# Wider table rows, idle TensorE products ahead of the first batch, and a new order of all steps in a graph-attention kernel

## The chip, the cores and the metric

The kernel runs on one core of one Trainium2 chip. The metric is the device time of one execution in microseconds (us); lower is better. Engines are named as in the profile: PE is TensorE (PEld its weight loads), DVE is VectorE, ACT is ScalarE, POOL is GpSimd and SP is SyncE, which here only issues DMAs.

## The reference

The input x is (32, 512, 1024): 32 batches of 512 channels by 1024 nodes, in float32. adj is a 512 x 512 matrix. Cut to what matters:

```python
# layer 0: attention over the nodes
h = relu(layernorm(x))                            # over the 1024 nodes
q = einsum('c,bcn->bn', wq, h); k = einsum('c,bcn->bn', wk, h)
scores = q[:, None, :] + k[:, :, None]            # (b, m, n)
scores = where(scores > 0, scores, 0.01 * scores)
att = softmax(scores, axis=-1)
agg = einsum('bcn,bmn->bcm', h, att)
x = x + relu(einsum('oc,bcm->bom', adj, agg) + bm[None, :, None])
# layer 1: graph convolution over the channels
h = relu(layernorm(x))
x = x + einsum('bnf,nm->bmf', h, adj * adj) + bias
```

## The kernel before

A score is one number of the row plus one of the column, with a kink at zero. So the kernel never forms the 1024 x 1024 scores. It sorts the nodes by q and keeps running sums of weighted values over the sorted nodes. For each column it then looks up where the kink falls, and joins two running sums. The work of one batch goes through these steps, each a small function:

- load (L578) brings the four x tiles of 128 x 1024. stats, norm, slopes and relu make h of layer 0.
- scores (L625) makes q and k (tile pq). It writes q to DRAM (qd), and row reads it back onto all partitions (qrow). columns (L641, L646) turns q and k into columns (pr, qk).
- rank (L667 to L676, on DVE) counts for every node how many q lie below it. lower (L683, on ACT) finds for every column where its kink falls. to_rows and from_rows make table rows of these numbers, and factors makes the exponents.
- value (L724) multiplies h by the turned adjacency (wmT) into tile pv, spread copies pv to SBUF (v, L731). scatter, on POOL, adds one column with q (L736) and writes the 128 rows of v to their sorted places in a table in DRAM (td, L737, indirect DMA).
- fetch (L753) reads the sorted rows back (vs). weights, later, totals and stationary make the weights (w, wc, e, den, sm; the products pd at L785 and L786).
- scan (L812, L809) makes running sums of the sorted rows in nine pieces (sc). sums carries the last row of a piece into the next ones (vs, L821, L822) and copies the piece with its column of den to t (L824, L825), which SP writes into the table (L827, L828).
- gather (L833, POOL, indirect DMA) fetches for every column three neighbouring table rows (g). excess, divide, weigh and combine (L842 to L862) join them. turn (L869, L871) transposes the result (tr) and adds it to a fresh copy of x that reload (L583) brought (y).
- stats, norm, slopes, relu and lift handle layer 1. propagate (L876) multiplies by the squared adjacency (wsq, tile pg), and finish (L884, L888) adds and writes out.

Steps of up to six batches are in flight at once, and the order in which they are issued is written out. PLAN gives every step of a batch a time, FIRST and LAST shift and stretch these times for the first and the last six batches. Batch s.b adds s.b x T, with T = 80.647:

```python
shift, stretch = FIRST[name][s.b]
t = s.b * T + t + shift + stretch * (t - mean)
...
steps.sort(key=lambda e: e[:2])
with tc.manual_schedule():
    for _, _, f, args in steps:
        f(*args)
```

These times only sort; no engine waits for them. Every engine and every DMA queue takes its instructions in the resulting order. The setup steps run once: adjacency loads adj, turn_adjacency (L533, tile pt) transposes it and ACT copies it to wmT (L534), square makes wsq on POOL, and pads fills the table places that no node takes. ident, the identity for transposes, is made by POOL at the very start. TABLES = 5 tables are used in turn, and each table row has W = C + 1 = 513 floats, 512 values and one more for q or den. PSUM has 8 banks of 128 x 512 floats, handed out in turn by bank().

Of the kernel before, what the change touches and what calls it, by code (L numbers as in the profile page):

```python
# [16 lines left out]
P = 128  # L17
# [6 lines left out]
FAR = -1.0e30  # L24
# [4 lines left out]
    "adjacency": (-988.26,),  # L29
    "biases": (-98.417,),  # L30
    "columns": (-36.55,),
    "combine": (
        258.562, 258.888, 261.232, 259.873, 259.273, 258.008, 255.401, 254.706, 263.584, 262.603,
        263.336, 256.739, 262.598, 262.619, 257.172, 258.38,
    ),
    "compare_mask": (-790.92,),
    "divide": (245.486,),
    "excess": (235.359,),
    "factors": (7.808,),
    "fetch": (33.445,),  # L40
    "finish": (320.504, 328.605, 338.372, 339.335, 347.583, 375.553, 352.541, 377.322),
    "from_rows": (59.35,),
    "gather": (219.377, 220.155, 219.449, 220.224, 220.347, 220.229, 219.664, 221.598),
    "later": (44.625,),
    "lift": (323.119, 320.65, 321.319, 325.518),
    "load0": (-153.915,),
    "load1": (-113.779,),
    "load2": (-165.384,),
    "load3": (-89.604,),
    "lower": (-8.757, 10.345, -12.887, -23.448, -21.118, -20.974, -1.148, 2.379),  # L50
    "masks": (-130.916,),
    "norm0": (-78.759,),
    "norm1": (284.555,),
    "pads": (-161.502, -74.73, -204.361, 23.867, -54.392),
    "propagate": (312.313, 317.412, 326.151, 316.354, 335.303, 344.312, 335.972, 347.511),
    "rank": (-14.187, -14.293, -17.198, -17.342, -15.511, -15.036, -11.325, -13.895),
    "reload0": (192.65,),
    "reload1": (238.382,),
    "reload2": (232.99,),
    "reload3": (257.454,),  # L60
    "relu0": (-61.287, -58.703, -61.202, -57.828),
    "relu1": (301.878, 303.027, 301.741, 302.05),
    "row": (-36.021,),
    "scan": (51.176, 57.633, 64.219, 81.673, 97.074, 108.292, 133.694, 146.062, 161.601),
    "scatter": (20.023, 15.884, 17.044, 17.539, 21.356, 19.535, 20.598, 20.763),
    "scores": (-41.613,),
    "slopes0": (-64.705,),
    "slopes1": (285.486,),
    "spread": (-28.707, -25.435, -27.151, -16.385, -9.829, -20.617, -16.323, -10.067),
    "square": (-559.865,),  # L70
    "stationary": (45.131, 68.681, 108.55),
    "stats0": (-97.083, -80.936, -91.631, -79.428),
    "stats1": (279.045, 280.054, 279.907, 280.042),
    "sums": (51.891, 59.593, 72.069, 86.019, 99.75, 116.792, 139.403, 150.307, 173.296),
    "to_rows": (-11.86, -7.955),
    "totals": (50.392,),
    "turn0": (264.575, 264.492, 264.401, 264.843),
    "turn1": (269.122, 269.027, 269.324, 268.845),
    "turn_adjacency": (-328.788,),
    "value": (-34.236, -39.683, -34.816, -23.667, -14.904, -27.47, -22.782, -17.741),  # L80
    "weigh": (250.503, 251.121, 249.656, 248.481, 251.121, 249.301, 250.914, 250.078),
    "weights": (41.352,),
# [3 lines left out]
        (-34.664, 0.5139), (-50.924, 3.8424), (-25.352, -0.3814), (5.756, -0.7592),  # L86
        (-3.834, -3.5685), (-13.836, 0.3613),
    ),
    "combine": (
        (-10.962, -0.1119), (-1.308, -0.1439), (3.109, -1.7623), (9.89, 2.7475), (4.44, -0.7933),  # L90
        (2.961, -1.451),
    ),
    "divide": (
        (-6.347, -0.8568), (2.891, -3.3805), (-4.843, -2.2912), (-14.719, 0.1095), (0.139, -0.7459),
        (-4.639, -1.4913),
    ),
    "excess": (
        (3.406, 3.0798), (0.53, -2.1584), (-5.407, -3.6123), (-5.253, 0.2855), (1.538, 1.0506),
        (-3.02, -0.7059),
    ),  # L100
    "factors": (
        (-39.948, -1.434), (8.997, -3.1502), (-4.905, 1.5535), (21.711, -1.2202), (-25.661, 2.8879),
        (13.506, 1.2709),
    ),
    "fetch": (
        (-7.266, -0.8474), (-8.348, -0.3577), (-7.803, -0.4204), (-12.929, 0.9352),
        (-3.76, -1.7209), (-5.744, 2.9838),
    ),
    "finish": (
        (-8.493, -0.4813), (6.16, 0.0186), (3.358, -0.186), (-1.573, -0.1421), (1.288, 0.2274),  # L110
        (-7.871, -0.1255),
    ),
    "from_rows": (
        (-0.341, 2.1537), (116.48, -0.09), (-35.198, 1.4406), (-25.171, -1.3726), (0.332, 0.6924),
        (-16.655, 0.2663),
    ),
    "gather": (
        (-5.507, 0.5725), (-4.646, -0.3848), (-17.558, -0.6343), (-8.351, -0.483), (5.293, 1.8179),
        (-2.911, -0.6571),
    ),  # L120
    "later": (
        (-10.16, 1.3573), (-2.311, -1.2079), (-2.744, 1.4084), (-11.928, 2.0169), (-8.624, -2.2893),
        (0.485, -2.4426),
    ),
    "lift": (
        (-13.784, -1.0616), (3.658, -0.7922), (-29.558, 1.5668), (-5.824, -1.5872), (1.316, 0.2108),
        (-13.838, -1.4015),
    ),
    "load0": (
        (-175.071, -1.0804), (-56.257, 0.2897), (-197.902, -2.8166), (2.16, -0.6659),  # L130
        (-45.079, 1.0239), (23.433, -0.0172),
    ),
    "load1": (
        (-99.914, 2.1645), (-71.298, -3.9416), (-78.407, 2.8558), (-85.073, 0.4063),
        (-18.406, -0.1573), (-28.218, 0.3374),
    ),
    "load2": (
        (-70.747, -1.2538), (-111.83, -0.5989), (-26.701, -0.4923), (-111.109, -0.0099),
        (-20.511, 0.9791), (15.469, 0.2457),
    ),  # L140
    "load3": (
        (-206.722, 1.2803), (-128.427, -0.9745), (-37.172, 1.9538), (-74.142, 0.1775),
        (-13.958, 1.1538), (-37.508, 0.7277),
    ),
    "lower": (
        (-27.213, -0.696), (-36.917, 0.5414), (-27.222, -0.2022), (-13.712, -0.526),
        (-10.212, -0.0938), (46.957, -1.0187),
    ),
    "norm0": (
        (-82.445, 1.5089), (-65.85, -1.4094), (-21.204, -0.8537), (-14.029, -0.5842), (1.32, 1.776),  # L150
        (1.134, -0.2082),
    ),
    "norm1": (
        (-3.753, -0.8553), (7.036, 1.1487), (-3.41, 0.1137), (10.96, 0.1134), (5.687, 1.1579),
        (-1.719, -1.6549),
    ),
    "propagate": (
        (-0.512, -0.1834), (1.688, 0.0269), (-2.93, -0.0228), (-0.493, -0.1178), (0.476, -0.1272),
        (0.797, -0.0815),
    ),  # L160
    "rank": (
        (-18.998, 0.7993), (-32.202, -0.2074), (-19.965, 1.145), (-3.668, -1.203),
        (-5.408, -1.0875), (2.158, -0.1924),
    ),
    "reload0": (
        (-78.853, -1.3542), (-2.901, -0.2085), (48.545, 0.1436), (11.898, 1.3227),
        (28.811, -1.2219), (-1.29, -0.8095),
    ),
    "reload1": (
        (-41.749, 0.1112), (-10.749, -0.6043), (11.812, -1.0105), (7.019, -0.2259),  # L170
        (-60.814, -0.4054), (-89.384, 1.1482),
    ),
    "reload2": (
        (5.935, 0.7012), (9.237, 1.9026), (-112.445, -1.6665), (29.821, 0.2364), (-22.535, -0.3722),
        (10.909, 1.7943),
    ),
    "reload3": (
        (-10.61, -1.1804), (-7.721, -1.5967), (-28.859, -3.3307), (-19.113, 0.0501),
        (-9.413, 0.4983), (-16.835, 0.7363),
    ),  # L180
    "relu0": (
        (-60.02, 1.4731), (-66.989, -0.4028), (-18.196, 0.1369), (-19.764, 0.0603), (3.168, 0.0151),
        (-1.522, 0.1367),
    ),
    "relu1": (
        (-11.851, 2.5102), (-0.995, 1.8084), (-17.155, -2.1914), (1.666, 2.1743), (4.982, -0.4455),
        (3.476, 0.1775),
    ),
    "row": (
        (-58.902, 0.8165), (-32.755, -3.2129), (-16.685, -0.2803), (-0.884, 2.3638),  # L190
        (-10.929, 0.751), (-15.002, 1.1386),
    ),
    "scan": (
        (-5.392, -0.0092), (-4.281, 0.0691), (-9.753, -0.1007), (-4.67, 0.0238), (-1.515, -0.0228),
        (-2.326, 0.0007),
    ),
    "scatter": (
        (-9.248, -0.2038), (-2.595, 1.766), (5.273, -0.6066), (-14.049, -0.0507), (0.917, 1.0603),
        (-5.17, -0.1987),
    ),  # L200
    "scores": (
        (-62.678, -1.1751), (-58.023, -2.2273), (-24.037, 0.8897), (-9.373, 1.8513),
        (-9.692, 0.3259), (-10.3, 1.643),
    ),
    "slopes0": (
        (-59.101, 0.4464), (-71.353, -1.9588), (-30.833, -0.0625), (-22.09, 0.6177),
        (-7.677, 1.4505), (-7.382, -0.8102),
    ),
    "slopes1": (
        (-1.669, -0.6445), (12.184, -1.231), (-2.177, 0.2468), (12.041, 0.2135), (12.134, -1.0604),  # L210
        (1.475, -1.9438),
    ),
    "spread": (
        (1.755, 1.4749), (-14.586, -0.2764), (13.174, 0.6637), (10.836, 0.3786), (3.075, 0.789),
        (3.759, 0.7174),
    ),
    "stationary": (
        (-7.431, 0.0753), (2.851, 0.1776), (-11.126, -0.3907), (-4.759, 0.0962), (-1.682, 0.227),
        (-1.878, -0.1006),
# [224 lines left out]
def kernel(  # L444
# [32 lines left out]
    nc = tc.nc  # L477
    B, C, N = x.shape
# [89 lines left out]
    def bank(name):  # L568
        return ps.tile([P, HALF], F32, tag="bank", name=name)
# [401 lines left out]
```

## Time and profile before

| | |
|---|---|
| median of 3 runs | 2365.21 us (2362.98 to 2367.83) |
| the profiled execution | 2365.35 us, of which 2363.6 us are the span of its instructions |
| mean granted TensorE clock | 0.987 |
| busy, share of the span | PE 97%, DVE 83%, ACT 61%, POOL 31% |
| DMA | 643.59 MB, 272 GB/s on average; queue q1 (SP) 355.90 MB, q0 (POOL, indirect) 268.99 MB |
| chain that ended last | PE 78%, DVE 8%, DMA 7%, ACT 3% |

Lines of a timeline give the start and the length in us, the engine, the line of the kernel, the operation, the tile written and those read, and how many records. In brackets stands how long the engine sat idle before and what ended that. A product of float32 shows as two records, a transpose as one. Matmuls overlap, so the busy time of PE is not PE at its peak. The granted clock is the share of TensorE's full clock that the throttle let through.

### The profile page before, as it was taken

The page shows a single profiled execution, that of the slowest core. Times are in us where ns is not written, and L with a number is a line of the kernel's source. Part 1 is how long each engine was busy: PE and PEld are TensorE (multiplying, and loading weights), DVE is VectorE, ACT ScalarE, POOL GpSimd, SP SyncE. Part 2 cuts the span into 40 slices and gives each one's busy share as a digit, 9 for nine tenths or more (in the row PEclk, how much of TensorE's full clock was granted, in tenths as well). Part 3 has the DMA queues.
Part 4 walks back from the last instruction along what each step waited for, and adds up shares of the span by engine and source line. Part 5 has one row for each costly group of instructions (what it writes and reads, how often), then busy time and mean ns, then how long its engine had stood idle before and what let it go on. Part 6 is the DMA issues. An engine that isn't in the chain of part 4 may idle for free.

```text
span 2363.6 us, 27844 instructions
## 1 busy us (share of the span) xinstructions
PE 2290.4 (97%) x7568; PEld 1006.6 (43%) x7568; DVE 1954.1 (83%) x4981; ACT 1441.9 (61%) x2821; POOL 734.0 (31%) x971
## 2 busy tenths in 40 slices
PE   7898999999999999999999999999999999999997
PEld 3333444444444444444444444444444444444443
DVE  6557887898988888988888888888988896899875
ACT  4666666655766655666665666665676556676530
POOL 2233333233233223233323233323233333334310
PEclk8998999999999999999999999999999999999998
DMA  5779987988988898998898998889897898788971
GB/s 186 234 214 286 270 267 251 324 275 246 303 289 274 298 295 262 289 289 284 296 295 263 276 299 279 292 298 264 272 304 257 294 305 271 252 270 285 323 291 71
DMA packets 205356, 643.59 MB, mean 272 GB/s; under 512 B 27504, under 2 KB 27632, under 8 KB 205200
## 3 DMA queue, kind: packets, MB, share of 16 engines
q1 hardware_dynamic: 141408, 355.90, 50.6%
q0 software_dynamic: 57344, 268.99, 31.8%
q10 hardware_dynamic: 6448, 16.92, 2.2%
q8 instruction: 61, 1.00, 0.2%
q14 instruction: 95, 0.78, 0.1%
HBM read 429.94 MB, written 211.77 MB: 271 GB/s over the span
## 4 chain that ended last, share of the span: by engine, by line
PE 78%; DVE 8%; DMA 7%; ACT 3%; POOL 1%; issue 1%; SPq 0%; ACTq 0%; DVEq 0%; POOLq 0%
PE pg L876 31%; PE pv L724 31%; PE sc L812 8%; PE tr L869 4%; PE pq L625 2%; DMA vs<-td 2%; DVE st L591 2%; DMA g<-td,idg 1%; DVE g L862 1%; ACT junk L683 1%; DMA td<-t 1%; PE sc L809 1%; DMA td<-v,idx 1%; DVE junk L672 1%; ACT h L613 1%
## 5 line engine op out<-in xcount | busy, mean ns | idle before, releaser
L724 PE MATMUL pv<-wmT,x 128*128 128x512 f32 x2048 | 920.8, 601 | 0.7 <-DVE step L602 0.7
L876 PE MATMUL pg<-h,wsq 128*128 128x512 f32 x2048 | 907.0, 596 | 14.0 <-ACT h L613 12.8
L876 PEld LDWEIGHTS pg<-h,wsq 128*128 128x128 f32 x2048 | 385.0, 191 | 508.3 <-issue 466.7
L724 PEld LDWEIGHTS pv<-wmT,x 128*128 128x128 f32 x2048 | 378.9, 191 | 509.3 <-issue 445.3
L796 POOL TENSOR_TENSOR sm<-mask_a,wc 128x192 f32<-128x192 f32 x96 | 55.4, 577 | 1150.2 <-DVE wc L773 814.6
L862 DVE SCALAR_TENSOR_TENSOR g<-g,cf 128x512 f32<-128x512 f32 x512 | 360.5, 760 | 13.5 <-ACT g L858 10.8
L821 ACT COPY vs<-sc 1x512 f32<-1x512 f32 x256 | 145.6, 569 | 355.8 <-PE sc L812 285.6
L737 POOL DMA_INDIRECT td<-v,idx x256 | 281.5, 1100 | 247.2 <-POOL v L736 46.4
L683 ACT ACTIVATE junk<-qrow,qk 128x1024 uint8<-128x1024 f32 x256 | 294.0, 1149 | 11.5 <-DMA qrow<-qd 9.6
L833 POOL DMA_INDIRECT g<-td,idg x256 | 243.7, 952 | 123.0 <-issue 72.7
L812 PE MATMUL sc<-vs,sm 128*64 128x512 f32 x1024 | 268.9, 616 | 10.2 <-ACT vs L821 5.6
L884 DVE SCALAR_TENSOR_TENSOR y<-pg,bm_sb,y 128x512 f32<-128x512 f32 x256 | 186.2, 741 | 44.4 <-PE pg L876 30.0
L871 DVE SCALAR_TENSOR_TENSOR y<-tr,nbm,y 128x512 f32<-128x512 f32 x256 | 174.6, 744 | 32.5 <-PE tr L869 30.9
L824 ACT COPY t<-sc 128x512 f32<-128x512 f32 x288 | 168.3, 585 | 38.3 <-DMA td<-t 32.6
L672 DVE TENSOR_SCALAR_CACHE_REDUCE junk<-qrow,qk,cnt 128x512 uint8<-128x512 f32 (+6 forms) x224 | 180.5, 806 | 8.2
L667 DVE TENSOR_SCALAR_CACHE_REDUCE junk<-qrow,qk 128x512 uint8<-128x512 f32 (+6 forms) x224 | 165.4, 738 | 21.7 <-DMA qrow<-qd 16.7
L591 DVE BATCH_NORM_STATS2 st<-x 128x6 f32<-128x512 f32 x256 | 163.1, 679 | 19.6 <-DMA x<-in_x_dram 19.4
L858 ACT ACTIVATE g<-g,cf 128x512 f32<-128x512 f32 x256 | 163.3, 712 | 3.4 <-DVE cf L852 3.4
L613 ACT ACTIVATE h<-y,nmr,rstd 128x1024 f32<-128x1024 f32 x128 | 151.7, 1234 | 17.9 <-DMA out_dram<-y 8.3
L619 DVE TENSOR_TENSOR y<-y,bias_sb 128x1024 f32<-128x1024 f32 x128 | 151.2, 1213 | 11.7 <-ACT h L613 11.5
L591 DVE BATCH_NORM_STATS2 st<-y 128x6 f32<-128x512 f32 x256 | 159.4, 665 | 0.0
L613 ACT ACTIVATE x<-x,nmr,rstd 128x1024 f32<-128x1024 f32 x128 | 149.6, 1233 | 7.6 <-DVE nmr L606 5.6
(102 smaller groups left out, 1771.0 us busy)
## 6 DMA issues: line engine op xcount, KB each, us to landing
vs<-td SPq DMA_DIRECT2D x96, 769.5 KB
td<-t SPq DMA_DIRECT2D x576, 128.2 KB
x<-in_x_dram SPq DMA_DIRECT2D x128, 512.0 KB
y<-in_x_dram SPq DMA_DIRECT2D x128, 512.0 KB
out_dram<-y SPq DMA_DIRECT2D x128, 512.0 KB
qrow<-qd ACTq DMA_DIRECT2D x32, 512.0 KB
td<-v,idx POOLq DMA_INDIRECT x256, 8.7
g<-td,idg POOLq DMA_INDIRECT x256, 12.6
```

Source lines behind the costliest of these rows:

```text
L591: nc.vector.bn_stats(st[:, i, :], s.x[c][:, ts(i, HALF)])
L613: nc.scalar.activation(h, s.x[c], AF.Relu, bias=s.nmr[:, c : c + 1], scale=s.rstd[:, c : c + 1])
L672: nc.vector.tensor_scalar(junk[:, j * P :], s.qrow[:, j * P :], qc, first, ALU.is_lt, ALU.add, accum_out=s.cnt[:, 1, j : j + 1],)
L683: nc.scalar.activation(junk, s.qrow, AF.Sign, bias=s.qk[:, 1, j : j + 1], accum_out=s.sgn[:, j : j + 1])
L724: nc.tensor.matmul(pv, s.h[c][:, ts(j, P)], wmT[:, c, :], start=(c == 0), stop=(c == NC - 1))
L737: i = nc.gpsimd.indirect_dma_start(tds[s.b % TABLES][:, :], bass.IndirectOffsetOnAxis(ap=s.idx[j // 4][:, j % 4 : j % 4 + 1], axis=0), v[: ...
L812: nc.tensor.matmul(p[ts(k, HP), :], m[:, k, :], s.vs[h][:, 0:C], start=True, stop=True)
L833: nc.gpsimd.indirect_dma_start(s.g[:, j, :], None, tds[s.b % TABLES].rearrange("(s k) w -> s k w", k=3), bass.IndirectOffsetOnAxis(ap=s.id ...
L862: nc.vector.scalar_tensor_tensor(r, s.g[:, j, k * W : k * W + C], s.cf[:, k, j : j + 1], r, ALU.mult, ALU.add)
L871: nc.vector.scalar_tensor_tensor(xh, pt, nbm[:, o : o + 1], xh, ALU.max, ALU.add)
L876: nc.tensor.matmul(pg, wsq[:, r, ts(c, P)], s.h[r][:, ts(i, HALF)], start=(r == 0), stop=(r == NC - 1),)
L884: nc.vector.scalar_tensor_tensor(xh, s.pg.pop((c, i)), bm_sb[:, c : c + 1], xh, ALU.add, ALU.add)
```

## The change

Three things change together.

W grows from C + 1 to C + 16, so that a table row has 528 floats and not 513. The added column becomes 16 equal columns wherever it is written (scatter, sums, pads). Reads of the last column of a row go by W, and stay as they were.

A new step, warm, multiplies the identity by itself eight times into a PSUM bank that nothing reads. PLAN has 14 such steps for the first batch.

All times of PLAN, FIRST and LAST are new, and with them the order on every engine; T stays.

```diff
 PLAN = {
...
+    "warm": (
+        -421.38, -325.504, -324.923, -278.205, -401.325, -283.603, -446.755, -384.541, -408.928,
+        -357.515, -265.475, -478.89, -371.765, -281.21,
+    ),
...
-    "scatter": (20.023, 15.884, 17.044, 17.539, 21.356, 19.535, 20.598, 20.763),
+    "scatter": (0.353, 1.616, 0.962, 8.013, 11.499, 6.907, 7.672, 11.834),
...
-    W = C + 1
+    W = C + 16
...
+    def warm(s, i):
+        pw = bank(f"pw_{i}")
+        for k in range(8):
+            nc.tensor.matmul(pw[:, 0:P], ident, ident, start=True, stop=True)
+
...
-        nc.vector.memset(pad[:, C : C + 1], FAR)
+        nc.vector.memset(pad[:, C:W], FAR)
...
-        nc.gpsimd.tensor_copy(v[:, C:W], s.qk[:, 0, j : j + 1])
+        nc.gpsimd.tensor_copy(v[:, C:W], s.qk[:, 0, j : j + 1].broadcast_to([P, W - C]))
...
-        nc.scalar.copy(t[:, C:W], s.den[:, i : i + 1])
+        nc.scalar.copy(t[:, C:W], s.den[:, i : i + 1].broadcast_to([P, W - C]))
...
             plan(s, pads, "pads")
+            plan(s, warm, "warm")
```

In the new order TensorE issues 8 of the warm steps, then the 16 transposes of the adjacency, then the other 6 warm steps, and then the scores of batch 0. For a batch in the middle, TensorE's groups (in matmul instructions) stand in this order, from one pq to the next:

```
before: pq16 pv4 pr2 pv8 pd4 sc4 pv8 sc2 pv8 sc4 pv4 pg12 sc4 pg12 sc1 pg4 tr16 pg4 tr16 sc2
after:  pq16 pv12 pr2 pd4 sc2 pv4 sc4 pv12 sc4 pv4 pg12 sc4 pg12 sc1 pg4 tr16 pg4 tr16 sc2
```

On the other engines the new order keeps the same steps per batch. DVE takes the slopes of layer 1 after the columns and not before them. ACT takes std of layer 1 ahead of the weights. SP issues fetch ahead of reload of the first tile. POOL issues the scatters some steps earlier. In the first batch DVE takes factors ahead of the ranks, and ACT takes six of the lower steps ahead of batch 1's relu.

## The prediction

> **What bounds the kernel now.** I read the granted clock and busy shares in stretches first, then TensorE's own timeline at the start and in the middle, then ScalarE's at the start. TensorE is busy for 97% of the span, so what counts is where it isn't. Columns: stretch, length, busy us (instructions) of PE, PEld, DVE, ACT, POOL, then granted clock, DMA share, GB/s.
>
> ```profile
> 13.27:26.92 13.65, 6.60 (x36) 2.43 (x37) 7.30 (x28) 5.51 (x7) 0.42 (x2) 0.50 0.74 255
> 26.92:80.00 53.08, 53.08 (x156) 23.40 (x156) 40.12 (x133) 28.77 (x54) 11.74 (x21) 1.00 0.56 173
> 80.00:250.00 170.00, 146.36 (x480) 58.08 (x476) 107.87 (x348) 116.09 (x239) 55.23 (x80) 0.92 0.83 254
> 250.00:500.00 250.00, 243.43 (x782) 107.30 (x778) 208.51 (x524) 158.00 (x307) 83.21 (x110) 0.99 0.85 268
> 500.00:1836.00 1336.00, 1335.44 (x4496) 590.35 (x4497) 1157.60 (x2946) 852.22 (x1673) 431.56 (x570) 1.00 0.90 284
> ...
> 2190.00:2363.00 173.00, 152.68 (x428) 67.52 (x426) 125.77 (x242) 59.06 (x109) 23.85 (x27) 0.95 0.62 226
> ```
>
> From 500 to 1836 us TensorE never rests: 19 batches of 70.2 us each, whatever the other engines do. Time can be won or lost in three places: the head (to 27 us), the ramp (80 to 500 us: 23.6 + 6.6 us idle, and 0.08 x 170 + 0.01 x 250 = 16 us lost to the halved clock), and the tail (20 us idle). The head on TensorE:
>
> ```profile
> 6.83 3.40 PE L533 MATMUL pt<-ident,adjn 128*128 128x128 f32 x16 [6.83 <-DMA adjn<-in_adj_dram]
> 19.14 1.08 PE L625 MATMUL pq<-x,wqk 128*32 128x256 f32 x8 [8.90 <-ACT x L613]
> 21.40 2.79 PE L625 MATMUL pq<-x,wqk 128*32 128x256 f32 x24 [1.18 <-ACT x L613]
> 24.11 5.08 PE L724 MATMUL pv<-wmT,x 128*128 128x512 f32 x8
> 29.03 0.38 PE L641 MATMUL pr<-ident,qr 128*128 128x128 f32 x2
> 29.24 20.77 PE L724 MATMUL pv<-wmT,x 128*128 128x512 f32 x48
> 49.94 1.93 PE L625 MATMUL pq<-x,wqk 128*32 128x256 f32 x32
> ```
>
> The first batch's scores (pq) wait for ScalarE's relu, and run at half clock. From 24.11 us on there is no gap: batch 1's scores at 49.94 stand behind 56 value records of batch 0, not behind data. So what moves the end of the first pq moves everything that follows on TensorE. And ScalarE ahead of it:
>
> ```profile
> 7.96 0.59 ACT L534 COPY wmT<-pt 128x512 f32<-128x512 f32 x1 [5.87 <-PE pt L533]
> ...
> 15.33 0.30 ACT L596 ACTIVATE std<-mv,eps_sb 128x4 f32<-128x4 f32 x1 [4.47 <-DVE mv L592]
> 15.66 0.20 ACT L598 ACTIVATE rstd<-std 128x4 f32<-128x4 f32 x1
> 17.84 4.63 ACT L613 ACTIVATE x<-x,nmr,rstd 128x1024 f32<-128x1024 f32 x4 [1.98 <-DMA td<-pad]
> ```
>
> The four copies of the turned weights sit ahead of std in ScalarE's queue. Today they are over long before it.
>
> **The change part by part.**
>
> *The idle products.* In the new order TensorE has 8 steps (64 products), then the 16 transposes of the adjacency, then 6 steps (48 products), and only then the first pq. They need only ident, ready at 1.5 us. What is one worth? No row shows it. From below: a 128x128 transpose, 1.75 us for 16 (the tr line at 848.85 to the next at 850.60), 0.11 us. From above: a float32 product is two records, and 24 records of 128x512 take 10.39 us (pg, 821.90 to 832.29), 0.866 us for each product, so 0.217 us for 128 columns. I take 0.217: these are products, and every product in the trace has two records. 112 x 0.217 = 24.3 us at full clock. The transposes of the trace ran at 3.40 / 16 = 0.21 us until 9.85, twice the full-clock 0.11, so the clock starts halved here too; some 3.4 us of work at half rate cost 1.7 us more. So: 1.5 + 64 x 0.217 + 1.7 = 17.1 us for the first transpose (now 6.83), 18.9 for the last, + 48 x 0.217 = 29.3 us for pq (now 19.14).
>
> Behind it on ScalarE: the copies of wmT end at about 18 + 4 x 0.6 = 20.2 instead of 10.9, std and rstd at 20.7, the slopes (0.8) at 21.5, relu (4.63) at 26.1. That is 3.6 us later than now but still hidden under the products, which end at 29.3; were the 6 later steps gone, relu would be the cost.
>
> What it gains: pq is unbroken, 1.9 us, and ends at 31.2 instead of 24.11 (+7.1); the first values take 3.5 us and not 4.92 (24.11 to 29.03), so the stream of values is +5.7 us behind. *The rule and the trace:* the row has 13.65 us at clock 0.50, with 6.60 us of TensorE work in them. The Trainium skill (TensorE: Matmul & The Clock Gate, "What's actually happening") has the gate open after one busy window of about 3.4 us and close after an idle one. By it, 3.4 us of products just ahead of pq buy all there is, and the 24.3 us put there speak against the change. By the row the most to be won is half of 6.60, 3.3 us; my step-by-step figure is 1.4 us in the values and about 1 in pq. By either, the work put in front outweighs it: **+5.7 us**, bounds -2.5 (a product at 0.11: 1.5 + 12.2 + 1.7 + 1.8 = 17.2 us, before relu is ready, so only the gain stays) and +8.
>
> *Rows of 528.* 15/513 = 2.9% more bytes in scatter, gather, vs and td: 269 MB on q0 and about 148 of q1, so 12.2 MB more of 644, 1.9%. In the steady part the DMA share goes from 0.90 to about 0.92, under TensorE's 1.00: nothing; without that cover it would be 1.3 us a batch. In the ramp, 170 x 0.83 x 0.019 = 2.7 us of transfers, part of it on the chain; in the tail two gathers of 15 us, 0.4 each. A row start could also become kinder to the DMA: the skill (DMA: Bandwidth & Descriptors, "How a descriptor splits into AXI transactions") charges for starts off 256 B. A gather starts at multiples of 4 rows, 8208 B now and 8448 = 33 x 256 B then; by that rule 6336 aligned bytes cost about what 6156 unaligned ones do, nothing instead of 2.9%. The trace's gather in the chain (15.16 us) can't tell. **+1 us**, bounds -3 and +4. The wider copies (16 columns on POOL, ACT and DVE where 1 was: ACT 0.19 us with 1 column, 0.20 with 8) are beside other work.
>
> *New times in the steady part.* The order per batch keeps every product; pr moves from behind one value group to behind three, next to pd. Now pv x8, pr, pv x16 take 3.54 + 0.21 + 6.97 us; an unbroken x24 group takes 10.39. That is -0.1 us or nothing, and the other groups are cut anew at 0.1 each: -0.05 x 19, **-1 us**, bounds -5 and +3. Cover checked: DVE's qk copy now waits for pr to 12.5 us after pq, but den waits to 13.05 there already (4.38 us idle); after it one y step fewer (0.67) stands before the combines that turn0 needs. qrow's read is behind the weights on ACT, as now; its last packet comes about 10.5 us after pq, before the ranks want it at 14. On SP the loads move only among td writes; fetch goes ahead of one reload; scatters on POOL start earlier.
>
> *New times in the ramp.* Followed by hand with the rows' durations: qrow of batch 0 lands 38 instead of 31.1; pq of batch 1 +5.6 (its relu, now behind six of the lower steps on ACT, is just in time); batch 0's scatters end +3; its first sc +5.5 (behind batch 1's values); pq of batch 2 +5; weights of batch 1 +4, since one lower step fewer is ahead of them on ACT; pq of batch 3 about 0, with 4.4 us of values moved behind it; weights of batch 2 +3 to +4. I take 1 us given back of the 5.7, bounds -15 and +8: 46 us of idle and half clock are at stake and I did not follow it past 200 us.
>
> *Tail.* The last 30 groups on TensorE are the same in both orders: 0, bounds -3 and +3.
>
> Sum: +5.7 + 1 - 1 - 1 = +4.7 on the profiled 2365.35 us (span 2363.6), which is the median of the runs, 2365.21, within 0.01%: **2370 us**.
>
> **The rivals.**
>
> 1. The head's delay arrives at the end (likeliest): 2370. For it: TensorE has no gap from 24 to 86 us that could take it up.
> 2. The ramp wins more than the head loses. Place: TensorE idle between 80 and 500 us. Price: a third of the 46 us, -15, against +5.7: 2355. It decides once the ramp gives back over 10 us. For it: all steps got new times, and each gap over about 3.4 us costs clock too. Against: the first 165 us, followed by hand, give back 2 or 3.
> 3. The delay vanishes in the ramp, as pq of batch 3 hints: about 2366.
> 4. A wait in the steady part: DVE ends the combines late, or pd waits for weights behind std on ACT. 0.5 us a batch are 10 us on top of 1: 2380. Against: the slack above.
> 5. The idle products cost half (0.11 us): the change does what it says and no more, 2362.
>
> **How the numbers follow.** Chances: 1: 0.46, 2: 0.22, 3: 0.12, 4: 0.13, 5: 0.07. About 0.2% (4.7 us) can be told from no change. Case 1 lies around that bound, two thirds beyond it on the slow side once its bounds (+8 in the head, +4 in the rows) are in; with 4 and their like this gives slower 0.55. Case 2 and a little of 3 and 5 give faster 0.27; the rest, 0.18, is within. Range 2353 to 2386: case 2 down to -12 and case 4 up to +20; case 1 alone 2364 to 2378.
>
> **What would show it.** Right: the first pq at about 29 us with clock 1.00, the adjacency's transposes at about 17, first values at about 31; PE full from about 550 to 1840 us with 70.1 to 70.2 us a batch. Wrong: pq at 19 to 21 (a product is cheap), PE idle in 80 to 500 under 20 us (rival 2), a period over 70.5 us (rival 4), or a gather in the tail's chain shorter than 15 us (the alignment pays).

## The result and the profile after

The change makes the kernel a little faster: median 2355.18 us (2350.76 to 2356.2, 6 runs) against 2362.93 us for the kernel before (2359.89 to 2367.83, 6 runs). The ratio is 0.9962 with a 95% interval of 0.9949 to 0.9975, so the gain is 0.25 to 0.51%, 6 to 12 us. The prediction's range just holds this time, near its lower end. Its likeliest case, 2370 us and slower, is wrong.

The granted clock and busy shares of the kernel after, in the stretches that the prediction showed of the kernel before (stretch, length, busy us and instructions of PE, PEld, DVE, ACT, POOL, then granted clock, DMA share, GB/s):

```profile
13.27:26.92 13.65, 13.65 (x125) 13.65 (x125) 6.08 (x19) 6.76 (x10) 0.00 (x0) 1.00 0.89 327
26.92:80.00 53.08, 53.08 (x212) 26.09 (x211) 41.95 (x136) 29.99 (x55) 10.29 (x18) 1.00 0.48 167
80.00:250.00 170.00, 152.78 (x514) 61.72 (x513) 115.21 (x370) 115.66 (x241) 58.80 (x89) 0.96 0.77 269
250.00:500.00 250.00, 248.65 (x847) 109.91 (x846) 215.69 (x530) 161.32 (x317) 71.77 (x105) 1.00 0.79 281
500.00:1836.00 1336.00, 1335.99 (x4488) 591.72 (x4487) 1158.36 (x2960) 856.30 (x1674) 432.70 (x570) 1.00 0.81 290
```

Two columns matter. TensorE's idle time from 80 to 500 us is 17.2 + 1.4 = 18.6 us where it was 23.6 + 6.6 = 30.2, and its clock from 80 to 250 us is 0.96 where it was 0.92. And the DMA share from 500 to 1836 us is 0.81 where it was 0.90, although the kernel moves 1.9% more bytes: the same traffic and more, in less DMA time. The prediction expected 0.92. The two traces lie further apart than the medians: their spans differ by 14.7 us and the medians by 7.8, since the traced execution of the kernel after (2350.76 us) was the fastest of its six and that of the kernel before (2365.35) was above its median. What follows splits up the 14.7.

The head on TensorE, in order of time (start, length, engine, line, tiles, records, idle before):

```profile
1.43 17.40 PE L532 MATMUL pw<-ident 128*128 128x128 f32 x128 [1.43 <-POOL ident masks.py:199]
18.67 1.91 PE L542 MATMUL pt<-ident,adjn 128*128 128x128 f32 x16
20.42 10.88 PE L532 MATMUL pw<-ident 128*128 128x128 f32 x96
31.23 1.93 PE L634 MATMUL pq<-x,wqk 128*32 128x256 f32 x32
33.09 3.70 PE L733 MATMUL pv<-wmT,x 128*128 128x512 f32 x8
...
36.85 20.77 PE L733 MATMUL pv<-wmT,x 128*128 128x512 f32 x48
```

The head is much as forecast: the long run of values starts 7.6 us later, at 36.85 us instead of 29.24. The ramp then wins back more than that. The page's shares of the chain that ended last, its queues, and its issues (packets, MB and share of 16 engines; then the median us from issue to landing) for the kernel after:

```profile
PE 87%; DVE 6%; DMA 3%; ACT 2%; issue 1%; POOL 0%; SPq 0%; ACTq 0%; DVEq 0%; POOLq 0%
...
q1 hardware_dynamic: 141408, 360.37, 45.1%
q0 software_dynamic: 57344, 276.86, 30.2%
...
td<-v,idx POOLq DMA_INDIRECT x256, 4.6
g<-td,idg POOLq DMA_INDIRECT x256, 11.8
```

The same lines of the page of the kernel before:

```profile
q1 hardware_dynamic: 141408, 355.90, 50.6%
q0 software_dynamic: 57344, 268.99, 31.8%
...
td<-v,idx POOLq DMA_INDIRECT x256, 8.7
g<-td,idg POOLq DMA_INDIRECT x256, 12.6
```

A scatter lands in 4.6 us instead of 8.7, and DMA's share of the chain falls from 7% (before) to 3%. Queue q1 moves more bytes in less time, and much of q1 has nothing to do with table rows: its 49,280 packets of 4096 bytes (x, y, the output and the bias) are the same in both kernels, and their mean time in the trace's packet records fell from 219 to 177 ns. So it isn't only the wider rows themselves that go faster. The new order has a part in this: with rows of 528 alone the mean was 192 ns, with the new order alone 201. Not all traffic went faster: the 4096 packets of qrow, on queue q10, rose from 201 to 254 ns.

The start of each batch's scores (pq), after minus before, from the two traces, shows where the time came from:

| batch | 0 | 1 | 2 | 3 | 4 | 5 | 6 | 8 | 10 to 24 | end of span |
|---|---|---|---|---|---|---|---|---|---|---|
| shift, us | +12.1 | +7.6 | +6.1 | -3.2 | -0.5 | -8.3 | -12.3 | -13.3 | -14.2 | -14.7 |

The ramp from batch 1 to batch 10 gives back 21.8 us, the steady part nothing and the tail half a microsecond. The stretches account for it: from 80 to 500 us TensorE is idle for 11.6 us less, and the halved clock costs about 9 us less, by an estimate from its shares (0.04 x 170 + 0.01 x 250).

### The profile page after: what moved, and what is told of

It reads as the page before. It is cut to its first block, busy times and chain, and to the rows that moved or that the text cites. A ratio compares the mean times of both kernels' runs of the same rounds, so it can differ in the third digit from the quotient of the medians.

```text
span 2348.9 us, 28244 instructions
## 1 busy us (share of the span) xinstructions
PE 2303.3 (98%) x7792; PEld 1028.4 (44%) x7792; DVE 1953.9 (83%) x4981; ACT 1446.0 (62%) x2821; POOL 721.9 (31%) x971
## 3 DMA queue, kind: packets, MB, share of 16 engines
q0 software_dynamic: 57344, 276.86, 30.2%
## 4 chain that ended last, share of the span: by engine, by line
PE 87%; DVE 6%; DMA 3%; ACT 2%; issue 1%; POOL 0%; SPq 0%; ACTq 0%; DVEq 0%; POOLq 0%
PE pv L733 35%; PE pg L885 34%; PE sc L821 9%; PE tr L878 4%; PE pq L634 2%; DVE g L871 1%; PE pw L532 1%; DVE st L600 1%; PE sc L818 1%; DVE y L880 1%; DMA td<-t 1%; DVE junk L681 1%; DMA g<-td,idg 1%; DMA qrow<-qd 1%; DVE junk L676 0%
## 5 line engine op out<-in xcount | busy, mean ns | idle before, releaser
L733 PE MATMUL pv<-wmT,x 128*128 128x512 f32 x2048 | 911.6, 598 | 0.0
L871 DVE SCALAR_TENSOR_TENSOR g<-g,cf 128x512 f32<-128x512 f32 x512 | 362.3, 762 | 18.2 <-ACT g L867 14.9
L746 POOL DMA_INDIRECT td<-v,idx x256 | 291.7, 1140 | 188.8 <-POOL v L745 41.2
L681 DVE TENSOR_SCALAR_CACHE_REDUCE junk<-qrow,qk,cnt 128x128 uint8<-128x128 f32 (+6 forms) x224 | 180.4, 805 | 8.2
L833 ACT COPY t<-sc 128x512 f32<-128x512 f32 x288 | 168.1, 584 | 17.8 <-DMA td<-t 11.6
L676 DVE TENSOR_SCALAR_CACHE_REDUCE junk<-qrow,qk 128x896 uint8<-128x896 f32 (+6 forms) x224 | 166.2, 742 | 11.2 <-DMA qrow<-qd 5.7
L740 ACT COPY v<-pv 128x512 f32<-128x512 f32 x256 | 142.6, 583 | 40.7 <-POOL sm L805 16.5
```

Source lines behind the costliest of these rows:

```text
L681: nc.vector.tensor_scalar(junk[:, j * P :], s.qrow[:, j * P :], qc, first, ALU.is_lt, ALU.add, accum_out=s.cnt[:, 1, j : j + 1],)
L733: nc.tensor.matmul(pv, s.h[c][:, ts(j, P)], wmT[:, c, :], start=(c == 0), stop=(c == NC - 1))
L746: i = nc.gpsimd.indirect_dma_start(tds[s.b % TABLES][:, :], bass.IndirectOffsetOnAxis(ap=s.idx[j // 4][:, j % 4 : j % 4 + 1], axis=0), v[: ...
L833: nc.scalar.copy(t[:, 0:C], p)
L871: nc.vector.scalar_tensor_tensor(r, s.g[:, j, k * W : k * W + C], s.cf[:, k, j : j + 1], r, ALU.mult, ALU.add)
```

## The experiments

The kernels of one comparison ran on one chip, beside the kernel before on that chip. There were five comparisons on five chips, so times of different comparisons are compared with care. "Rows of n" means a table row of n floats, with the added column written n - 512 times.

**First comparison: which part of the change does it (chip with before at 2359.09 us).** Theory A was that the wider rows speed up the DMA, since more of them start at multiples of 64 bytes, and that this shortens the ramp. The rival, theory B, was that the new order does it. Rows of 528 alone, in the order of before:

```diff
-    W = C + 1
+    W = C + 16
...
-        nc.gpsimd.tensor_copy(v[:, C:W], s.qk[:, 0, j : j + 1])
+        nc.gpsimd.tensor_copy(v[:, C:W], s.qk[:, 0, j : j + 1].broadcast_to([P, W - C]))
...
-        nc.scalar.copy(t[:, C:W], s.den[:, i : i + 1])
+        nc.scalar.copy(t[:, C:W], s.den[:, i : i + 1].broadcast_to([P, W - C]))
```

> The kernel before with rows of 528 floats, nothing else: old order, no idle products. Theory A (row starts: 2112 B is a multiple of 64, 2052 is not, and the DMAs beside table writes get quicker): DMA share in the middle falls from 0.90 to about 0.81, median time to landing of the table transfers from 10.0 to about 7.5 us, and the ramp shrinks: -8 to -15 us. Theory B (the new order alone fills the ramp): DMA may be quicker, but the time stays within 3 us of before, or is 1 to 2 us longer for 2.9% more bytes.

Measured: 2344.11 us, ratio 0.9933 (0.9918 to 0.9948), 15.0 us between the medians. The rows alone gain more than the whole change. Then the new order with rows of 513 and no idle steps, and the new order with rows of 528 and no idle steps:

```diff
-    W = C + 16
+    W = C + 1
...
-            plan(s, warm, "warm")
```

> The changed kernel with rows of 513 floats and without the idle products: the new order alone. Theory A: within 5 us of before, PE idle between 80 and 500 us about 25 to 30 us as before. Theory B: -15 to -20 us, PE idle there under 12 us.

Measured: 2354.98 us, ratio 0.9984 (0.9977 to 0.999).

```diff
-            plan(s, warm, "warm")
```

> The changed kernel without the idle products: new order and rows of 528. The value stream should start near 29 us as in the kernel before, 7.6 us ahead of the changed kernel. Theory 'the head is a cost that arrives': 5 to 8 us faster than the changed kernel, about -14 on before. Rival 'the ramp takes the head up' (the chain through DMA and ACT sets the ramp): within 2 us of the changed kernel. Second rival, the new order is tuned for a late start and stalls without it: slower than the changed kernel.

Measured: 2351.48 us, ratio 0.9967 (0.9954 to 0.998). On rows of 513 the new order gains 4.1 us between the medians, on rows of 528 it loses 7.4 (2351.48 against 2344.11). So the two gains don't add: in the order of before the rows bring 15.0 us, in the new order 3.5. Nor do the idle steps show at the end in the new order: without them its ratio is 0.9967, with them 0.9962 (and 0.9955 below), and the absolute times, of different chips, are 3.7 us apart. By the ratios the rival of this expectation holds, that the ramp takes the head up.

The new order with rows of 513 and no idle steps, from 80 to 500 us:

```profile
80.00:250.00 170.00, 148.84 (x496) 59.01 (x495) 110.40 (x353) 114.77 (x241) 57.12 (x87) 0.93 0.83 258
250.00:500.00 250.00, 248.70 (x846) 109.86 (x845) 214.49 (x528) 161.82 (x317) 73.72 (x107) 1.00 0.87 277
```

TensorE is idle for 21.2 + 1.3 = 22.5 us here. It was 30.2 in the trace of before (28.2 in a second one, on another chip), and it is 18.2 with rows of 528 alone and 18.6 in the kernel after. So the new order shortens the ramp too, though less. Last, the order of before with rows of 513 and the 14 idle steps:

```diff
+            plan(s, warm, "warm")
```

> The kernel before with the 14 steps of idle products at the same places among the setup steps, old order and rows of 513. Theory 'the head arrives': +5 to +8 us. Rival 'the ramp takes it up': within 2 us.

Measured: 2366.36 us, ratio 1.0033 (1.0021 to 1.0045): 7.3 us between the medians. This is nearly all of the 7.7 us by which its value stream is late, and so the prediction's first rival as it was described, in the order of before:

```profile
20.46 10.88 PE L532 MATMUL pw<-ident 128*128 128x128 f32 x96
31.28 1.93 PE L634 MATMUL pq<-x,wqk 128*32 128x256 f32 x32
...
36.90 20.77 PE L733 MATMUL pv<-wmT,x 128*128 128x512 f32 x48
```

Theory B falls as the main cause: the rows alone do more than the whole change, the new order alone about half of it. What the rows bring in the changed kernel itself, beside the new order and the idle steps together, was not measured; with rows of 513 that kernel did not run. How do faster transfers reach TensorE? ScalarE's groups from 80 to 360 us show it (busy us, mean ns, then idle time just before and what ended it). The kernel before:

```profile
L824 ACT COPY t<-sc 128x512 f32<-128x512 f32 x42 | 24.6, 586 | 7.3 <-DMA td<-t 6.5
...
L762 ACT ACTIVATE w<-vs,nq 128x3 f32<-128x3 f32 x12 | 3.5, 294 | 16.2 <-DMA vs<-td 16.2
```

Rows of 528 alone:

```profile
L824 ACT COPY t<-sc 128x512 f32<-128x512 f32 x43 | 25.1, 585 | 1.0
...
L762 ACT ACTIVATE w<-vs,nq 128x3 f32<-128x3 f32 x15 | 4.3, 290 | 5.7 <-DMA vs<-td 5.7
```

And the kernel after:

```profile
L833 ACT COPY t<-sc 128x512 f32<-128x512 f32 x42 | 24.6, 585 | 2.6 <-DMA td<-t 1.8
...
L771 ACT ACTIVATE w<-vs,nq 128x3 f32<-128x3 f32 x15 | 4.4, 292 | 8.8 <-DMA vs<-td 8.8
```

The new order alone, with rows of 513:

```profile
L833 ACT COPY t<-sc 128x512 f32<-128x512 f32 x42 | 24.6, 586 | 7.1 <-DMA td<-t 6.2
...
L771 ACT ACTIVATE w<-vs,nq 128x3 f32<-128x3 f32 x15 | 4.4, 292 | 15.4 <-DMA vs<-td 15.3
```

In the ramp ScalarE stands still for the weights until the sorted rows have come back from the table (16.2 us before, 5.7 with rows of 528), and for a free t until its write has landed (6.5 us, then no such wait). The new order alone leaves both waits about as they were, so its gain has another way, which was not followed. Behind the weights stand pd, and behind pd the running sums. In the same view TensorE's wait for w at pd falls with them; the kernel before, from 80 to 360 us:

```profile
L785 PE MATMUL pd<-w,mask_a 128*64 128x9 f32 x10 | 1.3, 203 | 7.3 <-ACT w L762 7.3
```

Rows of 528 alone:

```profile
L785 PE MATMUL pd<-w,mask_a 128*64 128x9 f32 x10 | 1.3, 206 | 3.1 <-ACT w L762 3.1
```

That is 4.2 of the 12.0 us by which TensorE's idle time from 80 to 500 us falls with the rows alone. The rest lies in smaller waits that were not followed one by one.

**Second comparison: is it where a row starts? (before at 2350.48 us).** Rows of 527 have nearly the bytes and copies of 528, but their starts are as uneven as those of 513. Rival C was that any wider row does it.

```diff
-    W = C + 1
+    W = C + 15        (and C + 8, and C + 4; the copies as with C + 16)
```

> The order of before, no idle products, rows of 527 floats: 2108 bytes, so nearly as many bytes and as wide copies of the added column as with 528, but only one row in 16 starts at a multiple of 64 bytes. Theory A (it is where a row starts that makes the DMA slow): no gain, ratio to before 0.999 to 1.002; DMA share 500 to 1836 us 0.89 to 0.91; table writes landing in 9 to 11 us. Rival C (any wider row does it: other banks, other sizes, wider copies on POOL and ACT): as with 528, ratio 0.992 to 0.995, DMA share 0.83, landing 7 us.

Measured: 2341.04 us, ratio 0.9962 (0.9948 to 0.9975).

> The order of before, rows of 520 floats: 2080 = 65 x 32 bytes, so half of the rows start at a multiple of 64 bytes and all at one of 32. Theory A with a grain of 64 bytes: between, about half of the gain of 528, ratio 0.996 to 0.998, DMA share 0.86. Theory A with a grain of 32 bytes: all of it, 0.992 to 0.995, share 0.82. Rival C (any wider row): 0.992 to 0.995 as well; it falls or stands by the rows of 527.

Measured: 2340.42 us, ratio 0.9956 (0.9943 to 0.997).

> The order of before, rows of 516 floats: 2064 = 129 x 16 bytes; all rows start at a multiple of 16 bytes, a quarter at one of 64. Theory A with a grain of 64: about a quarter of the gain, ratio 0.998; with a grain of 32: about half, 0.996 to 0.997; with a grain of 16: all of it, 0.992 to 0.995. Rival C (any wider row): 0.992 to 0.995.

Measured: 2341.34 us, ratio 0.9957 (0.9944 to 0.9971). DMA shares were 0.83, 0.82 and 0.83. The three are alike, so theory A falls: multiples of 64 bytes do nothing that can be measured here. A gather packet took 263 ns with rows of 527 (6324 bytes, uneven starts) and 264 with rows of 528 (6336 bytes, all starts at multiples of 64), by the packet records. The gain was smaller than with 528 before, because the kernel before was faster on this chip, and not because these kernels were slower.

The fourth kernel of this comparison has rows of 528 in the order of before, and only 8 idle steps, cut so that they end when the first scores could begin:

```diff
     "warm": (
-        (14 times)
+        (3 of them ahead of turn_adjacency, 5 behind it)
     ),
```

> The order of before, rows of 528 floats, and 8 instead of 14 idle steps: 3 ahead of the transposes of the adjacency and 5 behind them, 13.9 us at full clock, so that they end at about 19 us, when the first scores' input is ready. Theory (the gate is open for the first scores and values, and nothing is put back): the value stream starts 2 to 3 us earlier than with rows alone, and the end comes as much earlier: ratio 0.992 to 0.9925, against 0.9933 of rows alone. Rival (the ramp is set by DMA and swallows what the head gives): 0.993 to 0.994, as rows alone. Rival (the steps end late, at 21 us or more): 0.994 or above.

Measured: 2340.34 us (2337.74 to 2345.06), ratio 0.9961 (0.9947 to 0.9975). Its head does what was wanted:

```profile
10.37 9.10 PE L531 MATMUL pw<-ident 128*128 128x128 f32 x80
19.40 0.64 PE L633 MATMUL pq<-x,wqk 128*32 128x256 f32 x8
21.44 1.77 PE L633 MATMUL pq<-x,wqk 128*32 128x256 f32 x24 [1.40 <-ACT x L621]
...
26.89 20.77 PE L732 MATMUL pv<-wmT,x 128*128 128x512 f32 x48
```

The values start at 26.89 us, 2.35 earlier than before. But the median is within 1.0 us of the wider rows beside it that have no idle steps, and those differ by 0.9 among themselves. Whether this gain reaches the end is left open.

**Third comparison: how little is enough? (before at 2363.88 us).** A second copy of the kernel before, for its trace on this chip, and rows of 528, 515 and 514. Theory G was that rows of 513 are slow by themselves on every chip, rival H that the first trace of before was an unlucky one, and theory T that the 4 bytes beyond 2048 are the harm.

```diff
-    W = C + 1
+    W = C + 1         (then C + 16, C + 3, C + 2)
```

> The kernel of before once more, for its trace and its times on the same chip as the next three. The last comparison had before at 2350.5 us where the first had 2359.1. Theory G (a row of 513 is slow by itself, on every chip): ratio 1.000, DMA share 500 to 1836 us 0.87 to 0.90, table writes landing in 9 us or more, packets of 4104 bytes with a ninth decile over 290 ns. Rival H (the slow DMA of the first trace of before was its chip or its run): a share of 0.83 to 0.85 and landing at 7 to 8 us here.

Measured: 2363.48 us, ratio 0.9993 (0.9981 to 1.0005).

> The order of before, rows of 528 floats, on the same chip as before and as 515 and 514. Theory A as it was (multiples of 64 bytes) has fallen with 527. Theory G: ratio 0.993 to 0.997, DMA share 0.83. Rival H: ratio above 0.998.

Measured: 2340.69 us, ratio 0.9902 (0.9884 to 0.992).

> The order of before, rows of 515 floats (2060 bytes: 2048 and 12; starts at multiples of 4 bytes alone). Theory T (what is slow is the short tail of 4 bytes that a row of 513 has beyond 2048): fast like 516, ratio 0.993 to 0.997, DMA share 0.83, landing 7 us. Theory A with a small grain (8 or 16 bytes, 527 being fast for another reason): slow like before, 0.999 to 1.001.

Measured: 2341.93 us, ratio 0.9904 (0.9885 to 0.9923).

> The order of before, rows of 514 floats (2056 bytes: a tail of 8). Theory T with a tail of 4 bytes alone being slow: fast, 0.993 to 0.997. Theory T with tails under 12 or 16 bytes being slow: about 1.000, DMA share 0.88 or more.

Measured: 2342.99 us, ratio 0.9909 (0.989 to 0.9928). One float more per row gains 21 us, nine tenths of what 15 more do. From 500 to 1836 us, the copy of before:

```profile
500.00:1836.00 1336.00, 1335.51 (x4490) 590.16 (x4488) 1157.91 (x2946) 850.05 (x1670) 432.25 (x570) 1.00 0.89 284
```

Rows of 514:

```profile
500.00:1836.00 1336.00, 1335.01 (x4480) 588.88 (x4480) 1152.80 (x2934) 851.33 (x1672) 427.11 (x571) 1.00 0.84 284
```

The same 284 GB/s, at a share of 0.89 and of 0.84. Rows of 515 start no more evenly than rows of 513 (at any multiple of 4 bytes), and are as fast, at 0.83. Theory G stands and H falls.

**Fourth comparison: which transfer suffers? (before at 2365.41 us).** All of these have tables with rows 514 apart. First the fetches read only 513 floats of a row:

```diff
-            d = nc.sync.dma_start(t, sorted_rows(tds[s.b % TABLES], 3 * i, 3))
+            d = nc.sync.dma_start(
+                t[:, :, 0 : C + 1], sorted_rows(tds[s.b % TABLES], 3 * i, 3)[:, :, 0 : C + 1])
```

> Rows of 514 floats in the order of before, but fetch reads only the first 513 floats of each row (2052 bytes, as in before), and the last column isn't moved by it. Theory T-read (transfers that read rows of 2052 bytes are the slow ones): the gain of 514 falls away, ratio 0.998 or more. Theory T-write (it is the writes of rows of 2052 bytes, by scatter or by SP's copies of t): the gain stays, ratio as with 514 (0.990 to 0.996, by how slow before is on this chip), DMA share 0.83 to 0.84.

Measured: 2347.29 us, ratio 0.9918 (0.9903 to 0.9932), DMA share 0.84. Then SP writes only 513 floats of each row of t, and the last column of the tables is zeroed once in pads:

```diff
-        nc.sync.dma_start(td[ts(ha, HP), 0, :], t[0:HP, :])
-        nc.sync.dma_start(td[ts(hb, HP), 2, :], t[HP:P, :])
+        nc.sync.dma_start(td[ts(ha, HP), 0, 0 : C + 1], t[0:HP, 0 : C + 1])
+        nc.sync.dma_start(td[ts(hb, HP), 2, 0 : C + 1], t[HP:P, 0 : C + 1])
```

> Rows of 514 floats in the order of before, but SP writes only the first 513 floats of each row of t (2052 bytes, as in before); the last column of the tables is set to zero once, at the start. Theory T-write, by SP: the gain falls away, ratio 0.998 or more, DMA share 0.88. Theory T-write, by scatter (two rows of 2052 bytes to a packet of 4104), or T-read: the gain stays, ratio as with 514, share 0.84.

Measured: 2353.23 us, ratio 0.9942 (0.9925 to 0.9959), DMA share 0.84. The zeroing makes the scores of batch 2 start 7.9 us later than before; from there the ramp wins back 16.9 us, to -9.0 at batch 10. Neither brings the slow DMA back. On the same chip ran rows of 528 in the order of before with all 14 idle steps, and the changed kernel once more:

```diff
-    W = C + 1
+    W = C + 16
...
+            plan(s, warm, "warm")
```

> The order of before, rows of 528 and all 14 idle steps. If the head's delay of 7 to 8 us arrives, as it did with rows of 513: absolute time 2348 to 2350 us (rows of 528 alone gave 2341 to 2344). If the faster ramp swallows it, 2341 to 2344.

Measured: 2355.27 us, ratio 0.9956 (0.994 to 0.9972).

> The changed kernel once more, on the same chip as the other three. If rows of 528 are all that gains, and the idle steps and the new order cost: 2350 to 2355 us, slower than rows of 514 or 528 alone by 8 to 12 us. Rival (the difference between the comparisons is the chips'): within 3 us of the others.

Measured: 2355.24 us, ratio 0.9955 (0.9938 to 0.9971). The idle steps still cost with the fast DMA: 8.0 us against the narrow fetches on this chip, 11 us or more against rows of 528 on the others, which is beyond what was expected. And with the idle steps both orders end at the same time, so the 7.4 us that the new order loses without them are no loss beside them. Why that is stays open.

**Fifth comparison: the scatters, or the distance of the rows? (before at 2368.51 us).** The control has rows 514 apart, the fetches of 513, and the zeroing. The other kernel also writes just 513 floats with each scatter, by indices in floats instead of rows (the cut leaves out that the indices are multiplied by W, and that each table gets some rows more):

```diff
-            tds[s.b % TABLES][:, :],
-            bass.IndirectOffsetOnAxis(ap=s.idx[j // 4][:, j % 4 : j % 4 + 1], axis=0),
-            v[:, :], None,
+            fulls[s.b % TABLES].rearrange("n w -> (n w)").rearrange("(s k o) -> s k o", k=C + 1, o=1),
+            bass.IndirectOffsetOnAxis(ap=s.idx[j // 4][:, j % 4 : j % 4 + 1], axis=1),
+            v[:, 0 : C + 1], None,
```

> The control of the next kernel: rows of 514 floats in the order of before, fetch reads 513 floats of each row, SP writes all 514, the scatters write all 514; the last column of the tables is also set to zero once at the start, which held the head up by about 9 us where it was done before. Both theories: as there, 2350 to 2356 us, DMA share 500 to 1836 us 0.84, landing of a scatter about 4.6 us.

Measured: 2354.57 us, ratio 0.9944 (0.9931 to 0.9956).

> As the control, but each scatter writes only the first 513 floats of its rows (the table's rows stay 514 apart). Theory S (the scatters' rows of 2052 bytes make the DMA slow): slower than the control by 8 us or more, 2360 to 2372 us; DMA share 0.88 to 0.90; landing of a scatter about 8.7 us. Rival P (it is the distance of 2052 bytes between rows in the tables, for gathers and writes alike): within 3 us of the control, share 0.84, landing 4.6 us.

Measured: 2359.13 us, ratio 0.9961 (0.9948 to 0.9974). The time lies 4.6 us above the control, between the two expectations, but the DMA share tells them apart: 0.88 to 0.90 by theory S, 0.84 by its rival. The control from 500 to 1836 us:

```profile
500.00:1836.00 1336.00, 1335.09 (x4483) 588.88 (x4482) 1152.04 (x2938) 849.71 (x1668) 427.37 (x570) 1.00 0.84 284
```

The scatters of 513 floats:

```profile
500.00:1836.00 1336.00, 1334.92 (x4484) 588.87 (x4483) 1155.15 (x2942) 849.26 (x1667) 426.28 (x570) 1.00 0.85 284
```

A scatter packet of 4104 bytes (two rows of 513) took 178 ns on average here, with the rows 514 apart. It took 210 and 211 ns in the two traces of the kernel before, the same 4104 bytes with the rows 513 apart. The ramp gives back 16.2 us here (from +8.2 at batch 2 to -8.0 at batch 10) and 17.2 in the control (+6.8 to -10.4). Most of the difference in the profiled runs is there by batch 3 (+2.8 us), ahead of this. So theory S falls. What goes with the slow DMA is the width of 513 itself, not the bytes that a fetch, a write of t or a scatter moves when it alone is narrow. Theory T, that the 4 bytes beyond 2048 do the harm, falls with it for these three transfers one at a time; the gather was never narrowed. Three things grew together in every fast kernel and are not told apart: the distance of the rows in the tables, the width of the tiles in SBUF, and the length of a gather. A wider row can also move whatever is placed behind the tables in DRAM and behind the tiles in SBUF. In the last kernel each table had more rows, 2565 instead of 2304, and the DMA stayed fast; the rest of this rival was not tested. Why 513 is slow stays open.

## Why the prediction was wrong

**The rows of 528: the term that failed.** "+1 us, bounds -3 and +4" was -15.0 us between medians on one chip and -23.2 on another (2340.69 against 2363.88), for the rows alone in the order of before. In the new order it was -3.5. The step weighed bytes (1.9% more) and a rule of the Trainium skill (DMA: Bandwidth & Descriptors, "How a descriptor splits into AXI transactions"), which charges for starts off 256 B. The bytes don't show in the times here, and the rule doesn't explain the gain: 527 and 515, with uneven starts, do as well as 528, and a gather packet took 263 ns with 527 against 264 with 528. Its neighbour in the text, "the DMA share goes from 0.90 to about 0.92", came out at 0.81: a cost of DMA time per byte that the trace showed to be uneven all along. In the trace of before, one in ten packets of 4096 bytes took over 352 ns while the median took 159. That spread does not say that the row's width is behind it, but it shows packets of equal bytes with times over twofold apart, so the bytes, on which the bounds of -3 and +4 rested, did not fix the DMA time. The sign that the prediction gave for its other thought, a gather in the tail's chain shorter than 15 us, did not come either (15.43 us, 15.16 before); the gain came without it.

**The ramp: "1 us given back of the 5.7, bounds -15 and +8".** 21.8 us came back in the pair of traces. The step followed the new order by hand up to 165 us with the durations of before, so transfers kept their old landing times. Those changed: ScalarE's waits for w (16.2 to 8.8 us) and for t (6.5 to 1.8) shrank. The new order's own part is smaller: -4.1 us at the end on rows of 513, and a loss on rows of 528. What the text offered as the sign of rival 2, less than 20 us idle from 80 to 500 us, is what happened (18.6), and its 2355 us is the measured time. Its reason, the new times, is a part of the cause only: they alone leave 22.5 us idle and end at 0.9984 of before. That the number fits is luck.

**The idle products: right for the head, open for the end.** The first 64 products took 17.40 us: by the trace's records they started 0.43 us apart until 7.4 us and 0.22 apart after that, so about 6 us ran at the low clock where the sum had 3.4 (3.5 us in the trace of the 8 idle steps). In the second run a product took 10.88 / 48 = 0.227 us, against 0.217 taken. The transposes came at 18.67 us (17.1 forecast), pq at 31.23 (29.3). The value stream was 7.6 us late against 5.7 forecast, most of it the slower first products. The clock was 1.00 for the scores and values of batch 0, as said. Alone this step costs 7.3 us at the end, so the main case, that the head's delay arrives, holds where nothing else changes. In the new order it does not show, by the ratios 0.9967 without these products and 0.9962 with them; the absolute times, of different chips, leave at most 3.7 us of the 5.7 that the sum carried to the end. Rival 5, products at half the price, is out.

**The steady part: right.** 70.22 us a batch in both traces, against 70.2 and 70.1 to 70.2 forecast: the faster DMA gives nothing there, under TensorE's full 1335.99 of 1336 us. The -1 us did not show.

**The tail: right in size.** From -14.2 at batch 24 to -14.7 at the end. In the order of before, traces on two other chips with rows of 528 gain 2 to 5 us there.

So the sum was +4.7 by steps of which head, steady part and tail were off by some 3 us in all, in the pair of traces. The two steps that depend on how long a transfer takes, rows and ramp, came to 0 in the sum and to -21.8 us there; by the medians the miss is 7 us smaller.

## What to carry to other kernels

In this kernel the DMA was busy for 0.9 of the time, and that time did not follow the bytes: one float more per row took 0.05 off the share at the same GB/s. So ahead of forecasting what a wider or narrower row does, look at the spread of the packets' times in the trace. Where the ninth decile is twice the median, as here, a row one element wider is a one-line experiment; that such a spread tells as much in other kernels isn't shown.

A transfer that is hidden in the steady part may still set the ramp, where engines wait for single landings; its price is read there. Two changes that shorten the same ramp don't add: try each alone, and each beside the other. And products that only keep the clock up cost nearly all of their delay in the order of before, and nothing measurable where they ended when the data came.

## What the runs showed of the hardware

- A table row of 513 floats (2052 bytes) made the DMA slower than one of 514, 515, 516, 520, 527 or 528: share 0.89 to 0.90 against 0.82 to 0.84 in the order of before, at 284 to 290 GB/s. Other traffic suffered with it: the mean of q1's unchanged 4096-byte packets was 218 to 221 ns with 513, 204 with 514, 189 to 197 with 515 to 528. In the new order it was 201 with 513 and 177 to 179 with 528.
- How much it costs depends on the chip or the occasion: the kernel before stood at 2350.5, 2359.1, 2363.9, 2365.4 and 2368.5 us in the five comparisons, while rows of 514 to 528 in its order stood at 2340.3 to 2344.1 us in three of them (in the fourth, rows 514 apart with fetches of 513 at 2347.3). So one width's ratio was 0.9902 on one chip and 0.9933 on another.
- Rows of 514 to 528 in the order of before, without idle steps, beat both kernels: 2340.4 to 2344.1 us against 2355.2 and 2350.5 to 2368.5.
